# A four-layer graph network: one small product for two, later pair sums, kept loads on another queue, and half of a weight product at the end of the layer

## The chip, the cores and the metric

The kernel runs on one core of a Trainium2 chip. The metric is the time of one execution in microseconds (us) on the device. A core has TensorE (PE, matrix products; PEld is its weight load), VectorE (DVE), ScalarE (ACT), GpSimd (POOL) and SyncE (SP). The last two issue nearly all the transfers here; each engine works through its own queue in order, and waits at the head of it.

## What is computed

Four layers over a graph of N = 2708 nodes with F = 512 features; `adj` is dense with some 1.2% ones. Each layer is `x = layernorm(x + layer(x, adj))`. The change touches layer 0 and one product that layer 3 uses:

```
# layer 0, H = 4 heads of D = 128; both patterns are adj, so att has one mask
Xw  = einsum('hnd,hde->hne', Xh, W)
sig = sigmoid(f1[:, :, None] + f2[:, None, :])        # f1, f2: (H, N)
att = masked_softmax(adj * sig, adj != 0)             # (H, N, N)
Xa  = att @ Xw                                        # encode
Xn  = batchnorm(Xa as (N, F), gamma, beta)
emb = batchnorm(elu(Xn @ Wm.T + bm) + Xn)             # encoder MLP
Y   = elu((att @ emb) @ W.T)                          # decode, same att
out = batchnorm(elu(Y @ Wd.T + bd) + Y)               # decoder MLP
# layer 3
a = (x @ Wq + bq) @ (x @ Wk + bk).T / sqrt(512) + adj + adj
out = softmax(a) @ (x @ Wv + bv)
```

The kernel computes layer 3's scores from the merged weights `Wq Wk^T / sqrt(512)`, and it makes these within layer 0 and stores them to DRAM (`mqk_d`).

## The kernel before

**Tiles.** Features lie on 128 partitions in C = 4 chunks. The nodes are cut into NT = 22 blocks of up to 128 (the last has 20), and into two halves of 1354 columns, each in three parts of about 452 columns (a bank of PSUM takes 512). Heads go in two pairs.

**Attention passes.** `attention_pass` runs twice: encode (0 to about 572 us of the profile) and decode (about 693 to 1197 us). Each goes over half hf = 0, 1, over head pair p = 0, 1, and over the 22 blocks in the order `ORDER`. For each block the helper `form` loads the adjacency tile `a` (SP's queue, L358; 3 or 4 buffers), ScalarE makes the tanh of f1 + f2 for both heads of the pair (L385), VectorE multiplies with the mask (L393, one instruction of 128x2708), ScalarE takes the exponential (L394), and TensorE multiplies: six `po` products of 128x452 (L460). In encode, pass p = 0 also prepares the adjacency: VectorE makes `z` (tag z, one buffer, L374) and puts -1e30 where adj is 0 (L375), and GpSimd stores it to `adj_d`; the later passes load it from there. In decode VectorE counts the zeros of each column with another `z` (L335).

**Sums.** In encode TensorE also sums the exponentials over the nodes: `psm`, eight products of 128x340 (L483). For p = 1 most blocks are taken in pairs: VectorE adds two blocks' t (L477) and one `psm` does for both.

**Kept tiles.** Five block places of each pass (`KEPT`) have their finished `t` stored in DRAM in encode (GpSimd's queue, L442) and loaded again in decode in place of being formed (L445: 16 transfers of 1354 KB and 12 of 211.6 KB, on SP's queue). `t` has four buffers; a load waits until TensorE has read what the buffer held before.

**At a pass's end** (`keep`, in encode) the sums in PSUM are copied to `ft`, by VectorE and ScalarE in turn (L569). After pass (half 0, pair 1) `small_product` (L535 to L540) multiplies the encoder weights by the batch norm's beta: four products of 128x1 by 128x512, a copy of the row to SBUF (`row`, with the buffer of tag z), and four of 1x128 by 1x1, which turn it into a column; L575 adds the MLP's bias. Next to it VectorE clips the sums (L580), and the reciprocals go through DRAM (`few`, L589) and back as `rb`; the scaling and its statistics are done one by one behind the next pass's blocks.

**MLP stage** (about 572 to 693 us). Batch norm's scale and mean; wq and wk loaded and turned on TensorE (`tp_w`, L657); enc_w scaled in place (L677 on VectorE for two chunks, ScalarE for two); the sixteen products of the merged weights (L685, `ps_m`), copied to the tile `emb`'s free end by ScalarE and stored by GpSimd (L694); a small product `ps_u`; then for the six column chunks 4x4 products `ps_mlp` (L713), with a second small product `ps_mean` behind the first of them (the mean of the batch norm times the scaled weights, taken from the bias), elu (L499 to L508), and the turning of the result into rows (`tp_emb`, L745). Meanwhile the first decode blocks are formed, so VectorE has z and L393 of decode between the elus, and `linked` (L801), which needs the loads of `rb`.

**End of layer 0.** The last pass's sums go through `decode`'s tail: `ps_dec` (L848) and its elu; batch norm's scale and shift (L518 to L529, `bn_scale`, `bn_shift`). Layer 1 begins with a memset of one block of `hid_hi` (L955) and a copy of the centred weights (L965, `w_sb`), both ordered behind the shift; ScalarE applies the batch norm (L972), VectorE adds x (L979), TensorE turns the result (`tp_out`, L985) and multiplies (`ps_hid`, L117). Layer 1's tiles take the memory of layer 0's pools.

What is issued in which order is set by a list scheduler when the kernel is built, by each instruction's estimated readiness and the order of the program; `issue_after` puts a floor under it. The queues then run in that order.

Of the kernel before, what the change touches and what calls it, by code (L numbers as in the profile page):

```python
# [17 lines left out]
P = 128  # L18
# [11 lines left out]
def gnn_stack_kernel(  # L30
# [123 lines left out]
    mqk_d = dram.tile([C, P, C, P], F32, name="mqk_d")  # L154
    qscale = float(1.0 / F**0.5)
# [4 lines left out]
    with ExitStack() as l0:  # L160
# [160 lines left out]
        def attention_pass(values, first, att, psum, finish, f1b=None, blocks=(), spread=None, rest=None, taken={}):  # L321
# [83 lines left out]
            for hf, (h0, w) in enumerate(HSPAN):  # L405
                for p in range(H // HP):
# [13 lines left out]
                    before = None  # L420
                    for place, jt in enumerate(ORDER):
# [21 lines left out]
                        else:  # L443
                            for r in range(0, P if n == P else HB * Q, P if n == P else Q):
                                nc.sync.dma_start(t[r : r + n, :, :w], kept[:n, :, :w])  # L445
                            if p == 0 and jt in KEPT[1]:
                                count(hf, jt, att)
                        if po is None:


                            both = [
                                psum.tile([P, HP, BANK], F32, tag=f"po{q}", name="po", bufs=1)
                                for q in range(HB)
                            ]
                            po = [both[q][:, k, :] for k in range(HP) for q in range(HB)]
                        for k in range(HP):
                            h = HP * p + k
                            for q, (q0, qw) in enumerate(HCH[hf]):
                                r = 0 if n == P else q * Q
                                nc.tensor.matmul(  # L460
                                    po[HB * k + q][:, :qw],
                                    values[r : r + n, jt, h * P : (h + 1) * P],
                                    t[r : r + n, k, q0 : q0 + qw],
                                    start=(place == 0),
                                    stop=(place == NT - 1),
                                )
# [3 lines left out]
                        if prepare or not ALONE <= place < NT - LAST:  # L470
                            whole, m = t, n
                        elif place % 2 == 0:
                            before = t
                            continue
                        else:
                            whole, m = before, P
                            nc.vector.tensor_tensor(  # L477
                                whole[:n, :, :w], whole[:n, :, :w], tv, ALU.add
                            )
                        for k in range(HP):  # L480
                            for r, (q0, qw) in enumerate(SCH[hf]):

                                nc.tensor.matmul(  # L483
                                    sums[k][32 * r : 32 * r + 32, :SW],
                                    ones32[:m],
                                    whole[:m, k, q0 + qw - SW : q0 + qw],
                                    start=(place == 0),
                                    stop=(place == NT - 1),
                                )
# [62 lines left out]
        with (  # L552
# [8 lines left out]
            def keep(hf, p, po, sums):  # L561
# [10 lines left out]
                if hf == 0 and p == 1:  # L572
                    row = att.tile([P, HW], F32, tag="z", name="row", bufs=1)[:1, :F]
                    ps = small_product(po[0], mlp_w[0], prm_sb[:, B_ENC, :], row)
                    nc.vector.tensor_tensor(bias[:, 0, :], ps, prm_sb[:, MB_ENC, :], ALU.add)  # L575
# [55 lines left out]
            scale1, mean1 = batch_scale(stats, G_ENC, "bn1")  # L631

# [30 lines left out]
        with (  # L663
# [3 lines left out]

            (enc_w,) = mlp_w  # L670
            for c in range(C):
# [9 lines left out]
            mqk = emb[:, NT - 3 * C : NT - 2 * C, :]  # L681
            for c in range(C):
                ps = psum.tile([P, F], F32, tag="misc", name="ps_m", bufs=2)
                for o in range(C):
                    nc.tensor.matmul(  # L685
                        ps,
                        wqT[:, o, c * P : (c + 1) * P],
                        wkT[:, o, :],
                        start=(o == 0),
                        stop=(o == C - 1),  # L690
                    )
                nc.scalar.activation(mqk[:, c, :], ps, AF.Copy, scale=qscale)
            for o in range(C):
                nc.gpsimd.dma_start(mqk_d[o], mqk[:, :, o * P : (o + 1) * P])  # L694

            row = emb[:1, NT - 3 * C - 2 : NT - 3 * C, :]
# [8 lines left out]
            for ci, (c0, w) in enumerate(CHUNKS):  # L705
                pss = []
                for o in range(C):
# [13 lines left out]
                    if ci == 0 and o == 0:  # L721
                        pm = small_product(
                            psum.tile([P, F], F32, tag="misc", name="ps_mean", bufs=2),
                            enc_w,
                            mean1,
                            row[:, 1, :],
                        )
                        nc.vector.tensor_tensor(bias[:, 0, :], bias[:, 0, :], pm, ALU.subtract)
                        nc.vector.tensor_scalar(
                            bias[:, 1, :], bias[:, 0, :], 1.0, None, ALU.subtract  # L730
                        )
# [27 lines left out]
            spare = []  # L759

# [35 lines left out]
            def decode(hf, p, po, rb):  # L796
# [45 lines left out]
                def mlp(q, o, st, wide):  # L842
# [4 lines left out]
                    for c in range(C):  # L847
                        nc.tensor.matmul(  # L848
# [73 lines left out]
                for q in range(HB):  # L922
# [10 lines left out]
                    mlp(q, 3, st, True)  # L933

# [770 lines left out]
```

## Time and profile before

| | us |
|---|---|
| runs shown: median (lowest to highest of 3) | 3321.99 (3317.25 to 3322.62) |
| profiled execution: time | 3319.34 |
| profiled execution: span of the trace | 3317.5 |
| encode, 0 to 572: TensorE busy | 540.7 of 572 |
| MLP stage, 572 to 693 | 116.0 of 121 |
| decode, 693 to 1197 | 491.6 of 504 |
| layer 1, 1197 to 1510 | 304.3 of 313 |
| layers 2 and 3, to the end | 1780.1 of 1807.5 |

The span is the time from the first to the last instruction in the trace; 1.8 us of the execution lie around it. The granted clock of TensorE is 0.99 over the span. A row of a group reads: line, engine, operation, tile written and read, shapes, number; then busy time, mean ns of one; then idle time of the engine just before them and what ended it. A row of the waits reads: the engine and line that waited, what it waited for, us in all, times, the longest. A product in float32 stands as two records.

### The profile page before, as it was taken

The page shows a single profiled execution, that of the slowest core. Times are in us where ns is not written, and L with a number is a line of the kernel's source. Part 1 is how long each engine was busy: PE and PEld are TensorE (multiplying, and loading weights), DVE is VectorE, ACT ScalarE, POOL GpSimd, SP SyncE. Part 2 cuts the span into 40 slices and gives each one's busy share as a digit, 9 for nine tenths or more (in the row PEclk, how much of TensorE's full clock was granted, in tenths as well). Part 3 has the DMA queues.
Part 4 walks back from the last instruction along what each step waited for, and adds up shares of the span by engine and source line. Part 5 has one row for each costly group of instructions (what it writes and reads, how often), then busy time and mean ns, then how long its engine had stood idle before and what let it go on. Part 6 is the DMA issues. An engine that isn't in the chain of part 4 may idle for free.

```text
span 3317.5 us, 30401 instructions
## 1 busy us (share of the span) xinstructions
PE 3232.7 (97%) x10920; PEld 1725.2 (52%) x10920; DVE 1971.7 (59%) x3221; ACT 1319.5 (40%) x1497; POOL 130.1 (4%) x211
## 2 busy tenths in 40 slices
PE   8998999999999999999999999999999999999999
PEld 5443444454444446885554555444455555555554
DVE  7877977767687685445135667776353443543533
ACT  6887887457868652001133333332021010110111
POOL 1100100000000000000010000000000000000000
PEclk9999999999999999999999999999999999999999
DMA  8855863335555412540044444553211111111100
GB/s 289 299 189 169 310 214 123 105 108 199 177 176 175 161 40 84 144 123 15 1 127 128 119 124 134 148 148 108 69 46 34 42 34 42 40 32 45 36 24 20
DMA packets 172550, 381.45 MB, mean 115 GB/s; under 512 B 20938, under 2 KB 115094, under 8 KB 167982
## 3 DMA queue, kind: packets, MB, share of 16 engines
q1 hardware_dynamic: 156926, 308.16, 30.7%
q0 software_dynamic: 15472, 71.33, 5.8%
q8 instruction: 86, 1.41, 0.2%
q14 instruction: 66, 0.54, 0.1%
HBM read 307.22 MB, written 71.67 MB: 114 GB/s over the span
## 4 chain that ended last, share of the span: by engine, by line
PE 76%; DVE 9%; issue 8%; DMA 4%; ACT 3%; POOL 0%; SPq 0%; DVEq 0%; POOLq 0%; ACTq 0%
PE po L1310 22%; PE ps_s L1203 17%; PE po L460 11%; PE ps_nb L1044 6%; PE ps_wide L1105 4%; DVE t L393 3%; PE ps_hid L117 2%; PE ps_sup L1447 2%; PE ps_o L1388 2%; PE ps_mlp L713 2%; PE ps_dec L848 2%; DMA a<-adj_d 1%; ACT t L394 1%; DMA a_cols<-in_adjT_dram 1%; PE psm L483 1%
## 5 line engine op out<-in xcount | busy, mean ns | idle before, releaser
L393 DVE SCALAR_TENSOR_TENSOR t<-t,a 128x2708 f32<-128x2708 f32 (+1 forms) x156 | 462.1, 2974 | 125.0 <-ACT t L385 121.1
L385 ACT ACTIVATE t<-f1b,f2h 128x1354 f32<-128x1354 f32 (+1 forms) x312 | 428.1, 1413 | 61.7 <-PE po L460 28.0
L460 PE MATMUL po<-t,xw 128*128 128x452 f32 (+3 forms) x1056 | 415.1, 557 | 15.7 <-ACT t L394 15.7
L394 ACT ACTIVATE t<-t 128x2708 f32<-128x2708 f32 (+1 forms) x156 | 382.5, 2454 | 110.5 <-DVE t L393 110.3
L1310 PE MATMUL po<-sup,e 128*128 128x512 f32 x882 | 412.4, 602 | 6.2 <-DVE e L1500 5.9
L460 PE MATMUL po<-t,emb 128*128 128x452 f32 (+3 forms) x1056 | 400.3, 547 | 12.4 <-ACT t L394 9.1
L1310 PE MATMUL po<-e,xs 128*128 128x384 f32 (+1 forms) x1176 | 407.5, 489 | 0.0
L1203 PE MATMUL ps_s<-sup,hT 128*128 128x384 f32 (+1 forms) x1176 | 406.9, 490 | 0.0
L1581 DVE SCALAR_TENSOR_TENSOR e<-a_cols,ps_s 128x384 f32<-128x384 f32 (+1 forms) x154 | 85.6, 556 | 428.9 <-PE ps_s L1203 405.9
L460 PEld LDWEIGHTS po<-t,xw 128*128 128x128 f32 (+1 forms) x1056 | 191.2, 192 | 228.4 <-issue 201.7
L1203 PEld LDWEIGHTS ps_s<-sup,hT 128*128 128x128 f32 x1176 | 221.9, 190 | 164.2 <-issue 14.1
L460 PEld LDWEIGHTS po<-t,emb 128*128 128x128 f32 (+1 forms) x1056 | 193.5, 190 | 212.1 <-issue 187.3
L1310 PEld LDWEIGHTS po<-e,xs 128*128 128x128 f32 x1176 | 221.6, 190 | 157.2 <-issue 6.0
L1310 PEld LDWEIGHTS po<-sup,e 128*128 128x128 f32 x882 | 162.1, 192 | 173.9 <-issue 142.8
L1203 PE MATMUL ps_s<-hT 128*128 128x384 f32 (+5 forms) x672 | 212.3, 461 | 2.4 <-DVE e L1497 1.7
L97 ACT ACTIVATE ln_rstd<-ln_rstd 128x1 f32<-128x1 f32 x88 | 17.2, 201 | 495.0 <-DVE ln_rstd L96 494.7
L1496 ACT ACTIVATE a_cols<-a_cols,neg_big 128x384 f32<-128x384 f32 (+1 forms) x154 | 94.7, 616 | 239.0 <-DMA a_cols<-in_adjT_dram 190.7
L1044 PE MATMUL ps_nb<-hid_hi,at 128*128 128x512 f32 x484 | 185.6, 390 | 1.1 <-DVE at L1037 1.1
L1044 PE MATMUL ps_nb<-hid_lo,at 128*128 128x512 f32 x462 | 179.9, 389 | 0.0
L1305 DVE TENSOR_TENSOR acc<-acc,e 128x384 f32<-128x384 f32 (+2 forms) x294 | 162.4, 552 | 11.7 <-ACT e L1295 2.0
L1203 PEld LDWEIGHTS ps_s<-hT 128*128 128x128 f32 x672 | 122.4, 190 | 88.3 <-issue 17.3
L1294 DVE TENSOR_TENSOR e<-e,nmax 128x384 f32<-128x384 f32 (+1 forms) x308 | 154.5, 551 | 21.8 <-ACT nmax L1287 21.8
(247 smaller groups left out, 3316.8 us busy)
## 6 DMA issues: line engine op xcount, KB each, us to landing
a<-adj_d SPq DMA_DIRECT2D x110, 677.0 KB
a_cols<-in_adjT_dram SPq DMA_DIRECT2D x378, 192.0 KB
a<-in_adjT_dram SPq DMA_DIRECT2D x42, 677.0 KB
adj_d<-a POOLq DMA_DIRECT2D x42, 677.0 KB, 6.0
raw<-in_adjT_dram SPq DMA_DIRECT2D x105, 256.0 KB
kept<-t POOLq DMA_DIRECT2D x16, 1354.0 KB, 6.9
t<-kept SPq DMA_DIRECT2D x16, 1354.0 KB
a_cols<-in_adjT_dram SPq DMA_DIRECT2D x63, 202.0 KB
```

The costliest lines, as they stand in the source:

```text
L385: nc.scalar.activation(tv[:, k, :], f1b[:n, k, :w], AF.Tanh, bias=f2h[:n, jt, h : h + 1], scale=0.5,)
L393: step = nc.vector.scalar_tensor_tensor(tv, tv, GUARD, ab, ALU.add, ALU.mult)
L394: nc.scalar.activation(tv, tv, AF.Exp, scale=0.5)
L460: nc.tensor.matmul(po[HB * k + q][:, :qw], values[r : r + n, jt, h * P : (h + 1) * P], t[r : r + n, k, q0 : q0 + qw], start=(place == 0), ...
L1044: nc.tensor.matmul(pos[it], at, half[:, jt, :], start=(jt == 0 and k == 0), stop=(jt == NT - 1),)
L1105: nc.tensor.matmul(ps[:, :width], w(c, o), xt(c), start=(c == 0), stop=(c == C - 1),)
L1203: nc.tensor.matmul(ps[:, b * P : w], keys[:, c, j0 : j0 + P], st["q"][:, c, b * P :], start=(c == 0), stop=(c == C - 1),)
L1294: nc.vector.tensor_tensor(e, e, st["nmax"][:, :w], ALU.add)
L1305: nc.vector.tensor_tensor(acc, acc, e[:m], ALU.add)
L1310: nc.tensor.matmul(out, lhsT, rhs, start=(k == 0), stop=(k == NT - 1))
L1496: nc.scalar.activation(a, a, AF.Identity, bias=neg_big[: a.shape[0]], scale=1.0e30)
L1581: nc.vector.scalar_tensor_tensor(e, a, 2.0, ps, ALU.mult, ALU.add)
```

## The change

- The small product in `keep` goes, and `ps_mean` too. In their place one: `batch_shift` forms shift = beta - mean * scale of the encoder's batch norm, and `ps_shift` multiplies the weights with it, before they are scaled.
- The merged weights' products are in a helper, `merged(c)`. Chunks 0 and 1 of the four are made where all were. Then the turned weights wkT and half of wqT are stored to DRAM (`wkT_d`, `wqT_d`; 1 MB and 0.5 MB, GpSimd's queue). At the end of `decode` they are loaded into the two buffers of tag f1b (SP's queue), the other eight products go into two banks of `po` behind the last `ps_dec`, ScalarE copies them to a buffer of tag a, and GpSimd stores them to `mqk_d`, in four transfers of half the size.
- The loads of kept tiles are issued by GpSimd.
- The sums of a pair of blocks, and the addition before them, go into the helper `add_up`, which the program calls one block later: behind the next block's `form`, ahead of its `po` products.

```diff
--- before.py
+++ after.py
@@ -1,3 +1,4 @@
+from functools import partial
 from contextlib import ExitStack, nullcontext
 
 import concourse.bass as bass
@@ -152,6 +153,9 @@
     dram = ctx.enter_context(tc.tile_pool(name="dram", bufs=1, space=bass.MemoryType.DRAM))
     adj_d = dram.tile([N, N], F32, name="adj_d")
     mqk_d = dram.tile([C, P, C, P], F32, name="mqk_d")
+
+    wqT_d = dram.tile([P, C, C // 2 * P], F32, name="wqT_d")
+    wkT_d = dram.tile([P, C, F], F32, name="wkT_d")
     qscale = float(1.0 / F**0.5)
     uq = const.tile([P, C], F32, name="uq")
 
@@ -417,7 +421,7 @@
                     sums = None
                     if first and rest is None:
                         sums = sum_tiles()
-                    before = None
+                    before = waiting = None
                     for place, jt in enumerate(ORDER):
                         n = BLOCKS[jt][1]
 
@@ -442,7 +446,7 @@
                                 nc.gpsimd.dma_start(kept[:n, :, :w], tv)
                         else:
                             for r in range(0, P if n == P else HB * Q, P if n == P else Q):
-                                nc.sync.dma_start(t[r : r + n, :, :w], kept[:n, :, :w])
+                                nc.gpsimd.dma_start(t[r : r + n, :, :w], kept[:n, :, :w])
                             if p == 0 and jt in KEPT[1]:
                                 count(hf, jt, att)
                         if po is None:
@@ -453,6 +457,9 @@
                                 for q in range(HB)
                             ]
                             po = [both[q][:, k, :] for k in range(HP) for q in range(HB)]
+                        if waiting is not None:
+                            waiting()
+                            waiting = None
                         for k in range(HP):
                             h = HP * p + k
                             for q, (q0, qw) in enumerate(HCH[hf]):
@@ -467,26 +474,36 @@
                         if not first:
                             continue
 
-                        if prepare or not ALONE <= place < NT - LAST:
-                            whole, m = t, n
-                        elif place % 2 == 0:
+
+
+                        single = prepare or not ALONE <= place < NT - LAST
+                        if not single and place % 2 == 0:
                             before = t
                             continue
+
+                        def add_up(whole, m, more, first_one, last_one):
+                            if more is not None:
+                                nc.vector.tensor_tensor(
+                                    whole[: more.shape[0], :, :w],
+                                    whole[: more.shape[0], :, :w],
+                                    more,
+                                    ALU.add,
+                                )
+                            for k in range(HP):
+                                for r, (q0, qw) in enumerate(SCH[hf]):
+
+                                    nc.tensor.matmul(
+                                        sums[k][32 * r : 32 * r + 32, :SW],
+                                        ones32[:m],
+                                        whole[:m, k, q0 + qw - SW : q0 + qw],
+                                        start=first_one,
+                                        stop=last_one,
+                                    )
+
+                        if single:
+                            add_up(t, n, None, place == 0, place == NT - 1)
                         else:
-                            whole, m = before, P
-                            nc.vector.tensor_tensor(
-                                whole[:n, :, :w], whole[:n, :, :w], tv, ALU.add
-                            )
-                        for k in range(HP):
-                            for r, (q0, qw) in enumerate(SCH[hf]):
-
-                                nc.tensor.matmul(
-                                    sums[k][32 * r : 32 * r + 32, :SW],
-                                    ones32[:m],
-                                    whole[:m, k, q0 + qw - SW : q0 + qw],
-                                    start=(place == 0),
-                                    stop=(place == NT - 1),
-                                )
+                            waiting = partial(add_up, before, P, tv, False, False)
                     later += finish(hf, p, po, sums if first else rb) or []
             for work in later:
                 work()
@@ -569,10 +586,6 @@
                         taken[q % 2] = copy(
                             ft[:, HP * p + k, h0 + q0 : h0 + q0 + qw], po[HB * k + q][:, :qw]
                         )
-                if hf == 0 and p == 1:
-                    row = att.tile([P, HW], F32, tag="z", name="row", bufs=1)[:1, :F]
-                    ps = small_product(po[0], mlp_w[0], prm_sb[:, B_ENC, :], row)
-                    nc.vector.tensor_tensor(bias[:, 0, :], ps, prm_sb[:, MB_ENC, :], ALU.add)
                 sm = [att.tile([P, BW], F32, tag="rs", name="sm") for _ in range(HP)]
                 if not final:
                     for k in range(HP):
@@ -629,6 +642,7 @@
 
             attention_pass(xw, True, att, psum, keep, f1b, blocks, spread, rest, taken)
             scale1, mean1 = batch_scale(stats, G_ENC, "bn1")
+            shift1 = batch_shift(scale1, mean1, B_ENC, "bn1")
 
 
             emb = rows_tile("emb")
@@ -665,21 +679,9 @@
             tc.tile_pool(name="ps_c", bufs=1, space=PSUM) as psum,
         ):
 
-
-
-            (enc_w,) = mlp_w
-            for c in range(C):
-                if c % 2:
-                    nc.scalar.activation(
-                        enc_w[:, c, :], enc_w[:, c, :], AF.Copy, scale=scale1[:, c : c + 1]
-                    )
-                else:
-                    nc.vector.tensor_scalar(
-                        enc_w[:, c, :], enc_w[:, c, :], scale1[:, c : c + 1], None, ALU.mult
-                    )
-            stats = stats_tile("stats_b", NCH)
             mqk = emb[:, NT - 3 * C : NT - 2 * C, :]
-            for c in range(C):
+
+            def merged(c):
                 ps = psum.tile([P, F], F32, tag="misc", name="ps_m", bufs=2)
                 for o in range(C):
                     nc.tensor.matmul(
@@ -690,10 +692,38 @@
                         stop=(o == C - 1),
                     )
                 nc.scalar.activation(mqk[:, c, :], ps, AF.Copy, scale=qscale)
+
+            merged(0)
+
+
+            (enc_w,) = mlp_w
+
+            row = emb[:1, NT - 3 * C - 2 : NT - 3 * C, :]
+            pm = small_product(
+                psum.tile([P, F], F32, tag="misc", name="ps_shift", bufs=2),
+                enc_w,
+                shift1,
+                row[:, 1, :],
+            )
+            nc.vector.tensor_tensor(bias[:, 0, :], pm, prm_sb[:, MB_ENC, :], ALU.add)
+            nc.vector.tensor_scalar(bias[:, 1, :], bias[:, 0, :], 1.0, None, ALU.subtract)
+            for c in range(C):
+                if c % 2:
+                    nc.scalar.activation(
+                        enc_w[:, c, :], enc_w[:, c, :], AF.Copy, scale=scale1[:, c : c + 1]
+                    )
+                else:
+                    nc.vector.tensor_scalar(
+                        enc_w[:, c, :], enc_w[:, c, :], scale1[:, c : c + 1], None, ALU.mult
+                    )
+            stats = stats_tile("stats_b", NCH)
+            nc.gpsimd.dma_start(wkT_d, wkT)
+            nc.gpsimd.dma_start(wqT_d, wqT[:, :, half * P :])
+            merged(1)
             for o in range(C):
-                nc.gpsimd.dma_start(mqk_d[o], mqk[:, :, o * P : (o + 1) * P])
-
-            row = emb[:1, NT - 3 * C - 2 : NT - 3 * C, :]
+                nc.gpsimd.dma_start(
+                    mqk_d[o][:, :half, :], mqk[:, :half, o * P : (o + 1) * P]
+                )
             pu = small_product(
                 psum.tile([P, F], F32, tag="misc", name="ps_u", bufs=2),
                 wkT,
@@ -718,17 +748,6 @@
                             stop=(c == C - 1),
                         )
                     pss.append(ps)
-                    if ci == 0 and o == 0:
-                        pm = small_product(
-                            psum.tile([P, F], F32, tag="misc", name="ps_mean", bufs=2),
-                            enc_w,
-                            mean1,
-                            row[:, 1, :],
-                        )
-                        nc.vector.tensor_tensor(bias[:, 0, :], bias[:, 0, :], pm, ALU.subtract)
-                        nc.vector.tensor_scalar(
-                            bias[:, 1, :], bias[:, 0, :], 1.0, None, ALU.subtract
-                        )
                 for o in range(C):
                     dst = ft[:, o, c0 : c0 + w]
                     r = elu(
@@ -757,6 +776,7 @@
             dec_w = load_mlp(dec_wT, "dec_w")
             links = {}
             spare = []
+            last_dec = [None]
 
             def centre(pm):
 
@@ -845,7 +865,7 @@
                     q0, qw = HCH[hf][q]
                     ps = psum.tile([P, BANK], F32, tag="misc", name="ps_dec", bufs=2)
                     for c in range(C):
-                        nc.tensor.matmul(
+                        last_dec[0] = nc.tensor.matmul(
                             ps[:, :qw],
                             dec_w[:, c, o * P : (o + 1) * P],
                             t[:, c, q0 : q0 + qw],
@@ -931,6 +951,36 @@
                     if q == 0:
                         centre(po[0])
                     mlp(q, 3, st, True)
+
+
+                rest = [
+                    att.tile([P, HP, HW], F32, tag="f1b", name=name, bufs=2).rearrange(
+                        "p k w -> p (k w)"
+                    )
+                    for name in ("wk_again", "wq_again")
+                ]
+                wk_again = rest[0][:, : C * F].rearrange("p (c o) -> p c o", c=C)
+                wq_again = rest[1][:, : C * half * P].rearrange("p (c o) -> p c o", c=C)
+                nc.sync.dma_start(wk_again, wkT_d)
+                nc.sync.dma_start(wq_again, wqT_d)
+                mqk = att.tile([P, HW], F32, tag="a", name="mqk_rest", bufs=3)[:, : half * F]
+                mqk = mqk.rearrange("p (c o) -> p c o", c=half)
+                with tc.issue_after(last_dec[0].ins):
+                    for c in range(half):
+                        for o in range(C):
+                            nc.tensor.matmul(
+                                po[1 + c],
+                                wq_again[:, o, c * P : (c + 1) * P],
+                                wk_again[:, o, :],
+                                start=(o == 0),
+                                stop=(o == C - 1),
+                            )
+                for c in range(half):
+                    nc.scalar.activation(mqk[:, c, :], po[1 + c], AF.Copy, scale=qscale)
+                for o in range(C):
+                    nc.gpsimd.dma_start(
+                        mqk_d[o][:, half:, :], mqk[:, :, o * P : (o + 1) * P]
+                    )
 
             attention_pass(emb, False, att, psum, decode)
         dsum = small.tile([P, NT], F32, tag="dsum", name="dsum")
```

Lines of the changed kernel stand from 1 to 50 lines further down than those of the kernel before: L445 is L449, L460 is L467, L955 is L1005, L965 is L1015, L985 is L1035. `small_product` is as it was.

## The prediction

> **What bounds the kernel now.** I read the busy shares first, then the chain, then TensorE's waits, and then one window for each edit. The page's busy shares and its chain:
>
> ```profile
> PE 3232.7 (97%) x10920; PEld 1725.2 (52%) x10920; DVE 1971.7 (59%) x3221; ACT 1319.5 (40%) x1497; POOL 130.1 (4%) x211
> ...
> PE 76%; DVE 9%; issue 8%; DMA 4%; ACT 3%; POOL 0%; SPq 0%; DVEq 0%; POOLq 0%; ACTq 0%
> ```
>
> TensorE is busy for 3232.7 of 3317.5 us. So the change is worth what it takes out of TensorE's work, or out of the 85 us in which it is not busy, and nothing else counts. The list of TensorE's waits says where the larger pieces of those lie (time in all, times, longest):
>
> ```profile
> PE po L460 <- ACT t L394: 24.8, 13, 8.2
> PE tp_out L985 <- DVE ot L979: 7.5, 1, 7.5
> ...
> PE psm L483 <- DVE t L477: 3.7, 3, 1.4
> PE po L460 <- DVE ot L814: 3.2, 1, 3.2
> PE ps_u L540 <- DVE emb L538: 1.4, 1, 1.4
> ```
>
> Two waits stand out: 8.2 us for a masked exponential at a boundary between two passes (the first row's longest), and 7.5 us at the end of layer 0 (second row). The 3.7 us of pair sums are three waits.
>
> **1. The small product after pass (half 0, pair 1) goes.** TensorE's lines in the window 296 to 314 us:
>
> ```profile
> L460 PE MATMUL po<-t,xw 128*128 128x452 f32 (+1 forms) x8 | 4.3, 666 | 8.2 <-ACT t L394 8.2
> L535 PE MATMUL po<-enc_w,prm_sb 128*1 128x512 f32 x8 | 3.6, 592 | 0.0
> ...
> L540 PE MATMUL po<-ones,row 1*128 1x1 f32 x8 | 1.0, 248 | 0.8 <-DVE row L538 0.8
> ```
>
> The product occupies TensorE from 299.14 us, and the next pass's first po starts at 312.80: 3.6 + 0.8 + 1.0 + 8.2 = 13.7 us. VectorE is the reason for the 8.2. Its waits from 280 to 320 us:
>
> ```profile
> DVE ft L569 <- PE po L460: 9.5, 2, 9.2
> DVE row L538 <- PE po L535: 2.7, 1, 2.7
> ...
> DVE enc_bias L575 <- PE po L540: 1.1, 1, 1.1
> ```
>
> It sits idle 9.2 us for the old pass's sums, then 2.7 and 1.1 us inside the small product, and only then masks the new pass's adjacency (0.87 + 1.57 us) and multiplies (2.91 us): `row` has the only buffer of tag z, which the mask needs as well. Without `row` the build puts the first block's mask and product and the second's z ahead of the evacuations, into the 9.2 us. Its inputs are there: the tanh of two blocks ends at 288.8 us. Block 0 is then ready near 295 us, before TensorE's last old sum at 299.14. Later blocks cost VectorE 0.87 + 1.57 + 2.97 = 5.4 us, plus leftovers, against some 6.0 us on TensorE (its po and psm), so a stall of 0.5 to 1.5 us near the third or fourth is what I leave. The two other pass boundaries of this stage, at 172.9 and 445.1 us, show no gap. Gain 12 to 13.7 us at most; 8 if VectorE catches up slowly. I take **13 less 0.5 for late blocks: 12.5**. The replacement product of the shift (same 8 + 8 instructions) stands where `ps_mean`'s stood: no change in count.
>
> **2. Eight of the sixteen 128x512 products leave the MLP's start.** From 572 to 700 us the sixteen take 14.0 us (L685, 32 records, two to a product), so half is 7.0 us of TensorE's time. But VectorE is short of time there:
>
> ```profile
> DVE linked L801 <- DMA rb<-rs_d: 6.1, 1, 6.1
> DVE elu_r L506 <- ACT elu_m L501: 4.7, 5, 3.1
> DVE z L335 <- DMA a<-adj_d: 2.3, 1, 2.3
> ```
>
> Between 572 and 645 us it is busy 58.0 of 73, and its real slack appears only at 642 us (the 3.1). Products that start earlier meet a VectorE with the same 7 z, 4 multiplications of 2.97 us and the elus still to do, so the elus' evacuation holds the psum. Further, two new stores (1 MB and 0.5 MB, on GpSimd's queue) travel beside the loads that VectorE waits for here; by the page's rows a 1354 KB store takes 6.9 us to land and a 256 KB store 4.1, so I allow up to 2.5 us of delay for `linked` and z. The new shift product also makes the scaling of enc_w wait for a reader, 1.5 to 4 us later than before. Following both by hand: chunk 0's products end 5 us earlier, chunk 2's between 0.3 (loads late) and 3.3 us (not late) earlier. I take **2**, ends 0 and 3.5.
>
> **3. The same eight products return at the end of layer 0.** They fit into the wait of 7.5 us there: 8 x 0.87 = 7.0 us, directly behind the last ps_dec at 1197.3 us. So they cost nothing by themselves. What follows them does. Before, the timeline there reads:
>
> ```profile
> 1202.67 7.96 ACT L972 ACTIVATE ot<-ot,bn_shift,bn_scale 128x452 f32<-128x452 f32 x12 [0.84 <-DVE bn_shift L529]
> 1202.69 0.48 DVE L955 MEMSET hid_hi<- 128x512 f32 x1
> 1203.10 1.16 DVE L965 COPY w_sb<-xs 128x2048 f32<-128x2048 f32 x1
> 1204.17 3.85 DVE L979 TENSOR_TENSOR ot<-ot,xs 128x452 f32<-128x452 f32 x7
> ...
> 1204.84 0.47 PE L985 MATMUL tp_out<-ident,ot 128*128 128x128 f32 x1 [7.52 <-DVE ot L979]
> ```
>
> In the build of the changed kernel the memset waits for GpSimd's four last stores of mqk_d, because layer 1's tiles take the memory from which those stores read; the copy of the weights (w_sb) is queued behind it on VectorE, and ps_hid reads w_sb. The stores wait for two ScalarE copies out of po, the second behind four activations of L972 (0.66 us each): about 1205.9 us. Then four issues of some 0.65 us and a landing. The nearest rows are before's own four, issued from 602.42 to 604.38 and landed 605.74 to 611.15 us (median 4.1; 256 KB each, the new ones 128 KB), and the scores' stores (192 KB, 2.8). So the last lands at 1205.9 + 2.0 + 2.8..6.8 = 1210.7 to 1214.7, then 0.48 + 1.16, and ps_hid begins at 1212.4 to 1216.4 in place of 1205.2: 7.2 to 11.2 us late. The first transposes run meanwhile (0.4), and then VectorE's queue holds the row statistics behind the same memset, up to 2 us more. Layer 1's projection is bound by TensorE to 1490 us (no gap), so a delay is kept. I take **loss 8**. It could be nothing, if the stores are seen to have landed before the scale is ready, and 12 if the landing is slow and VectorE's backlog is the whole 2.
>
> **4. Kept loads move from SP's queue to GpSimd's** (16 of 1354 KB, 12 of 211.6 KB). SP's waits from 740 to 930 us:
>
> ```profile
> SPq L358 <- DVE t L393: 145.2, 28, 8.3
> SPq L445 <- PE po L460: 19.6, 4, 10.6
> ```
>
> A kept load waits for TensorE to free its t, and the adjacency loads behind it wait with it (19.6 us in four waits). VectorE in turn waits 19.1 us for such loads in that window, and TensorE loses 8.3 us to late exponentials there (5.8 at 795 us) and 3.2 at the evacuation L814, which stays. But at 784 to 796 us the adjacency load in front of the 5.8 waits for a multiplication (L393) to free its own buffer, not for a kept load; there the gain is only what earlier blocks bring. New costs: an issue on GpSimd takes 0.53 us (kept<-t, L442) where SP takes 0.32, and the landing, by the nearest row (6.9 us for a 1354 KB store from GpSimd), is longer than a block of the decode on TensorE; that is covered only because t has four buffers, so that a kept load can go out about three blocks ahead of its use. GpSimd has 1.05 us of work in the decode. I take **gain 3**, ends -3 (loads later) and +8.
>
> The Trainium skill speaks against this edit. "DMA: Bandwidth & Descriptors", section "Issuing engines are not separate DMA queues", says that transfers from all issuing engines share the same DMA engines and that a second issuer saves only the issue time. By that the edit is worth nothing on a path where SP's issue time is not late. The rows above show what that sentence leaves out: a queue whose head waits (10.6 us in one piece) holds what is behind it; so I keep a gain, but a small one. "SBUF — State Buffer" adds, in "The DVE blocks DMA trap", that descriptors made on GpSimd wait while VectorE runs a fast copy; no wait of that kind is in the rows of before.
>
> **5. Pair sums behind the next block.** The build has the same sequence of po and psm on TensorE in both kernels, and VectorE's additions in the same places but for the boundary. So the same three waits of psm for VectorE (3.7 us, shown at the top) stand where they stood: **0**; if they go after all, up to 3.7.
>
> **Sum**, against the profiled execution (3319.3 us; span 3317.5): -12.5 - 2 + 8 - 3 + 0 = -9.5, so 3309.8. The median of the runs shown is 3322.0, 2.7 above; I forecast **3310**, between the two bases (3309.8 and 3312.5).
>
> **Rivals.** (a) *The stall at the end is hidden*: the stores land before layer 1 asks, loss 0 to 2 in place of 8: 3319.3 - 12.5 - 2 + 1 - 3 = about 3303. For it: GpSimd is idle. Against: four stores behind a copy that is itself behind 2.6 us of activations. (b) *Nothing beside the boundary is gained*: VectorE gives back all of part 2 and the kept loads change nothing, and the end takes 9 to 10: 3319.3 - 12.5 + 9.5 = 3316. (c) *The other side*: kept loads on GpSimd's queue, whose head waits behind stores and copies of emb, arrive late. One late load stops TensorE for its excess over a block; 28 loads with 0.6 us each are 17 us, so 3310 + 3 + 17 = 3330. It decides from 0.4 us a load (11 us lost, 3324). (d) *The change doesn't do what it says* at pair sums: that is already in the sum, at 0; a gain there would give 3306.
>
> **How the numbers follow.** Forecast 0.45, (a) with (d) 0.25, (b) 0.17, (c) 0.13. A measurement of this kernel can tell about 0.2% (6.6 us) from no change. Faster holds the forecast, (a) and a small part of (b): 0.70. Same holds most of (b) and the mild end of (c): 0.18. Slower: 0.12. The range for 8 in 10 runs from 3298 (a with the kept loads' better end) to 3322 ((b) with both bad ends: 3319.3 - 12.5 + 12 + 3).
>
> **What would show it.** Right: no gap on TensorE from 299 to 312 us, first po of the pass right behind psm; memset of hid_hi 8 us or more after bn_shift with four mqk_d stores before it, and TensorE waiting there for w_sb; the row of SP's L445 gone; the elus of chunk 1 bound by VectorE. Wrong: a boundary that still waits for ACT t (then part 1 fails), or t of the kept blocks being waited for by TensorE (then part 4 has the wrong sign).

## The result, and the profile after

The change made the kernel slightly slower: 3329.11 us (median of 8 runs, 3327.89 to 3334.88) against 3322.13 (8 runs, 3317.25 to 3323.82), a ratio of 1.0027 with a 95% interval of 1.0016 to 1.0038. I had forecast 3310, in a range from 3298 to 3322.

TensorE's busy time hardly moved, and its waits did. First the page's busy shares, then the list of TensorE's waits of the changed kernel (us in all, times, longest):

```profile
PE 3232.2 (97%) x10904; PEld 1725.2 (52%) x10904; DVE 1972.2 (59%) x3221; ACT 1320.0 (40%) x1497; POOL 149.4 (4%) x245
```

```profile
PE po L467 <- ACT t L398: 40.8, 20, 6.6
PE ps_hid L118 <- DVE w_sb L1015: 5.5, 1, 5.5
...
PE psm L495 <- DVE t L486: 3.0, 3, 1.4
...
PE tp_out L1035 <- ACT mqk_rest L979: 1.7, 1, 1.7
```

The wait for ScalarE's exponential, which held the 8.2 us of the boundary before, did not shrink with it: it grew from 24.8 to 40.8 us. So waiting of that kind has come up somewhere else. The table says where; each entry is the length of a stage on TensorE in us, worked out from the starts and ends of its groups in the two traces.

| stage, by TensorE's own marks | before | after | difference |
|---|---|---|---|
| start to the last psm of encode | 572.3 | 557.5 | -14.8 |
| to the first po of decode (MLP stage) | 120.6 | 113.8 | -6.8 |
| to the last ps_dec (decode) | 504.4 | 530.9 | +26.5 |
| to the first ps_hid (change of layers) | 7.9 | 15.2 | +7.3 |
| to the last product | 2106.8 | 2103.5 | -3.3 |

The boundary's gap is gone. TensorE's lines in the window 296 to 314 us, after:

```profile
L467 PE MATMUL po<-t,xw 128*128 128x452 f32 (+1 forms) x37 | 15.0, 550 | 0.0
L495 PE MATMUL psm<-t,ones 128*32 128x340 f32 x48 | 4.1, 455 | 0.0
```

No small product stands between the passes, and the last column, the idle time before a group's instructions, is 0.0. But decode lost 26.5 us. VectorE's waits in decode, first in the kernel before, then after:

```profile
DVE t L393 <- ACT t L385: 78.1, 25, 5.7
DVE z L335 <- DMA a<-adj_d: 31.2, 13, 4.2
```

```profile
DVE z L339 <- DMA a<-adj_d: 76.9, 23, 8.5
DVE t L397 <- ACT t L389: 55.6, 17, 5.4
```

The count of zeros (z) waited 31 us for adjacency loads before, and 77 after. TensorE has no wait for a kept tile in its list: the kept loads, which were moved, are not late. What is late is the work of the blocks that are formed.

### The profile page after: what moved, and what is told of

It reads as the page before. It is cut to its first block, busy times and chain, and to the rows that moved or that the text cites. A ratio compares the mean times of both kernels' runs of the same rounds, so it can differ in the third digit from the quotient of the medians.

```text
span 3327.0 us, 30418 instructions
## 1 busy us (share of the span) xinstructions
PE 3232.2 (97%) x10904; PEld 1725.2 (52%) x10904; DVE 1972.2 (59%) x3221; ACT 1320.0 (40%) x1497; POOL 149.4 (4%) x245
## 4 chain that ended last, share of the span: by engine, by line
PE 59%; DVE 3%; DMA 1%; issue 0%; ACT 0%; SPq 0%; DVEq 0%; ACTq 0%
PE po L1360 22%; PE ps_s L1253 17%; PE ps_nb L1094 6%; PE ps_wide L1155 4%; PE ps_hid L118 2%; PE ps_sup L1497 2%; PE ps_o L1438 2%; DMA a_cols<-in_adjT_dram 1%; DVE e L1344 1%; PE tp L1145 0%; PE ps_s L1245 0%; DVE e L1550 0%; PE ps_parts L1277 0%; PE pb L1324 0%; DVE xs L1556 0%; DVE e L1547 0%
## 5 line engine op out<-in xcount | busy, mean ns | idle before, releaser
L397 DVE SCALAR_TENSOR_TENSOR t<-t,a 128x2708 f32<-128x2708 f32 (+1 forms) x156 | 461.8, 2975 | 104.7 <-ACT t L389 101.0
L467 PE MATMUL po<-t,emb 128*128 128x452 f32 (+3 forms) x1056 | 408.7, 555 | 30.5 <-ACT t L398 30.4
L398 ACT ACTIVATE t<-t 128x2708 f32<-128x2708 f32 (+1 forms) x156 | 382.5, 2454 | 114.1 <-DVE t L397 113.8
L467 PE MATMUL po<-t,xw 128*128 128x452 f32 (+3 forms) x1056 | 411.4, 552 | 10.5 <-ACT t L398 10.4
L467 PEld LDWEIGHTS po<-t,emb 128*128 128x128 f32 (+1 forms) x1056 | 197.0, 194 | 235.2 <-issue 191.8
L467 PEld LDWEIGHTS po<-t,xw 128*128 128x128 f32 (+1 forms) x1056 | 189.1, 190 | 221.6 <-issue 198.1
```

The costliest lines, as they stand in the source:

```text
L397: step = nc.vector.scalar_tensor_tensor(tv, tv, GUARD, ab, ALU.add, ALU.mult)
L398: nc.scalar.activation(tv, tv, AF.Exp, scale=0.5)
L467: nc.tensor.matmul(po[HB * k + q][:, :qw], values[r : r + n, jt, h * P : (h + 1) * P], t[r : r + n, k, q0 : q0 + qw], start=(place == 0), ...
```

## Experiments

Two theories stood after the traces. **A**: the kept loads on GpSimd's queue cost the 26.5 us. **B**: decode is paced by VectorE and the adjacency loads, so that the lead of 21.6 us which encode and MLP gave was lost there in any case. A splits in two: **A1**, the build orders VectorE's z and t otherwise when the loads are on that queue; **A2**, the transfers get in each other's way. In front of each diff stands the kernel that it starts from. The ratio is always to the kernel before on the same chip; the runs down to noend_pool were made on one chip and those from pool_order on another, so between the two groups ratios and stages are compared, not times.

No run undoes the later pair sums alone. In the traces, TensorE's order in the encode passes of noend_sp (below) and of the kernel before differs only around the small product, and psm waits for VectorE's additions 2.8 us in all, where it waited 3.7. So that part of the change did next to nothing.

**k_sp: the kept loads back on SP's queue.** From the changed kernel:

```diff
-                                nc.gpsimd.dma_start(t[r : r + n, :, :w], kept[:n, :, :w])
+                                nc.sync.dma_start(t[r : r + n, :, :w], kept[:n, :, :w])
```

> The changed kernel with the loads of kept tiles back on SP's queue, all else as changed. In the changed kernel the decode stage loses 26.5 us against before (TensorE stands 21.6 us ahead at the first po of decode and 4.9 behind at the last ps_dec). Theory A (the loads on GpSimd's queue are to blame, by the order of VectorE's work that the build makes with them or by the transfers): the decode loses 0 to 5 us, so the time is 3305 to 3310. Rival B (decode can't keep a lead, because VectorE and the loads of adjacency set its pace): it still loses 20 or more, time 3325 or more.

Measured: 3303.29 us, ratio 0.9959 (0.9946 to 0.9971), a little below what A gave. Decode takes 504.5 us, as before the change, and starts 19.6 us earlier than before. B falls: decode keeps a lead that it is handed.

**b_pool: the kernel before, with the one line the other way.**

> The kernel before with nothing but the loads of kept tiles moved to GpSimd's queue. Theory A: the decode gets 15 to 25 us longer, time 3337 to 3347. Rival B (decode gives back whatever lead it is handed): no lead is handed here, so within 5 us of before, 3317 to 3327.

Measured: 3341.42 us, ratio 1.0075 (1.0062 to 1.0088); decode 527.5 us, 23 more. The edit hands no lead over here, and the loss is nearly the same. A holds, and the line is enough by itself.

**noend_sp and noend_pool: all sixteen products of the merged weights at the start again.** From k_sp and from the changed kernel:

```diff
-            nc.gpsimd.dma_start(wkT_d, wkT)
-            nc.gpsimd.dma_start(wqT_d, wqT[:, :, half * P :])
-            merged(1)
+            for c in range(1, C):
+                merged(c)
...
-                wk_again = rest[0][:, : C * F].rearrange("p (c o) -> p c o", c=C)
...
```

> The changed kernel with the kept loads on SP's queue and all sixteen products of the merged weights at the start of the MLP stage: what is left of the change is the one small product for two and the pair sums. Against k_sp this undoes the move of half the products. Theory A2 (the move costs more at the end of layer 0 than it saves at the MLP stage, 7.3 us lost at the end and 6.8 saved at the start in the changed kernel): within 3 us of k_sp. Rival (the lead saved at the MLP stage is lost in decode, which the end then adds to): noend_sp is 5 us or more faster than k_sp, 3300 to 3305.

> The changed kernel with all sixteen products at the start of the MLP stage, the kept loads on GpSimd's queue. Theory A: the decode loss of some 20 us stays, since neither the MLP stage nor the end makes it: time 3322 to 3332. Rival C (the late decode comes from the two reloads of turned weights in SP's queue and the stores beside the decode's first loads): decode recovers, 3305 to 3312.

(A2 in the first of these two expectations stands for another theory, about the move of the products; elsewhere it is the transfers.) Measured: noend_sp 3306.30 us, ratio 0.9965 (0.9951 to 0.9979); noend_pool 3328.32, ratio 1.0033 (1.0020 to 1.0046). Their MLP stages are 120.4 and 120.3 us against k_sp's 113.3, and the change of layers 7.8 and 7.9 against 15.2: 7 us saved by the move, 7.3 lost. noend_sp is 3.0 us from k_sp, at the edge of what I gave for that. noend_pool's decode still takes 527.9 us, 23.5 more than before the change, so the reloads of the turned weights and the stores beside decode's first loads are not the cause of these. Since the pair sums did next to nothing, noend_sp is in effect the kernel before with one small product for two: 11.7 us faster by the medians.

**pool_order: GpSimd's queue, with VectorE's order of z and t held to SP's.** From the changed kernel; the list has 112 entries, the order of z and T in k_sp's build (T is the multiplication that writes t):

```diff
+DVE_ORDER = [
+    ('z', 0, 0),
+    ('T', 0, 0, 0),
...
+            if not first:
+                for u, v in zip(DVE_ORDER, DVE_ORDER[1:]):
+                    tc.add_manual_dep(
+                        made[v].ins,
+                        made[u].ins.name,
...
```

> The changed kernel, with the kept loads on GpSimd's queue as changed, but with VectorE's order of z and t (L339, L397) in decode held by hand to the order that the build makes with SP's loads (as in k_sp). Theory A1 (the loads on GpSimd lose time because the build gives VectorE another order of z and t, in which a z stands ahead of work that is ready and waits for its adjacency load): the decode loss goes, time 3303 to 3308, as k_sp's 3303. Rival A2 (the transfers themselves: kept loads that go out beside the adjacency loads slow these): the order does not help, 3322 to 3332.

Measured: 3307.83 us, ratio 0.9970 (0.9958 to 0.9981). The queue is the changed kernel's, and still decode takes 506.5 us instead of 530.9. VectorE's waits there:

```profile
DVE t L511 <- ACT t L503: 87.5, 27, 5.4
DVE z L453 <- DMA a<-adj_d: 25.2, 12, 4.0
```

The 77 us for adjacency are 25 again. With VectorE's order held, the build also sets ScalarE's order anew, but not in the first pass of decode (half 0, pair 0): there this trace and the changed kernel's have TensorE's, ScalarE's, GpSimd's and SP's instructions in the same order, and only VectorE's z and T differ. That pass takes 108.2 us, k_sp's 108.2 and the changed kernel's 118.4 (from its first po to the next pass's). So A1 is shown; of A2, with this order, there can be some 2 us in decode (506.5 against k_sp's 504.5), and that much is left.

**sp_order: the counterpart, SP's queue with the order of GpSimd's build.** The same edit on k_sp with the other list.

> The counterpart: k_sp (kept loads on SP's queue) with VectorE's order of z and t in decode held to the order that the build makes with GpSimd's loads. Theory A1: as slow as the changed kernel, 3322 to 3335. Rival A2: as k_sp, 3303 to 3308.

Measured: 3328.96 us, ratio 1.0038 (1.0025 to 1.0052), decode 531.7 us, as A1 said. It is the weaker of the two: its largest gap on TensorE (12.9 us at 725.6) has no match in the changed kernel, and SP's kept loads wait 89.1 us for TensorE, against 45.5 in k_sp. So here the order also works through SP's queue, and the equal total is partly chance.

**e_nostore: what makes the stall ahead of layer 1.** From k_sp, all sixteen products and stores at the start, and at the end:

```diff
-                for o in range(C):
-                    nc.gpsimd.dma_start(
-                        mqk_d[o][:, half:, :], mqk[:, :, o * P : (o + 1) * P]
-                    )
```

> k_sp with all sixteen products of the merged weights and their full stores at the start of the MLP stage, and the eight products at the end of layer 0 made a second time with their two copies by ScalarE, whose results are not stored. So it leaves out the four stores at the end, and TensorE makes eight products more in all. Theory: the stall ahead of layer 1 (15.2 us from the last ps_dec to the first ps_hid in k_sp, 7.9 in noend_sp) is the stores' landing, and goes to some 10 us without them; time 3306 + 2.5 = 3308 to 3310. Rival (the products and copies themselves make it): 13 to 15 us, time 3311 to 3314.

Measured: 3304.86 us, ratio 0.9966 (0.9953 to 0.9978), 10.4 us from the last ps_dec to the first ps_hid. The time is some 3 us below what I expected, less than the 4.4 us between this kernel's lowest and highest run; the stage is as expected. Of the 7.3 us lost, the stores make 4.8 (15.2 less 10.4) and the products and copies 2.6 (10.4 less 7.8).

**e_quarter: a quarter of the products at the end, in one store.** From k_sp (c = 3 alone, one copy, and):

```diff
+                nc.gpsimd.dma_start(
+                    mqk_d[:, :, C - 1, :].rearrange("o p j -> p o j"),
+                    mqk[:, 0, :].rearrange("p (o j) -> p o j", o=C),
+                )
```

> k_sp with a quarter instead of half of the merged weights at the end: four products of the sixteen, one copy by ScalarE ahead of the batch norm's scale, and one store in place of four. By the stall's arithmetic (copy at 4.1 us after the last ps_dec, one issue of 0.7, landing 2.3, memset and copy 1.6) ps_hid begins some 9 us after the last ps_dec, 1 later than without any product at the end, and the MLP stage is 3.4 shorter than noend_sp's: 2 us faster than noend_sp, about 3304, within 1 us of k_sp. Rival (the stall does not follow the stores): 14 us or more to ps_hid, 3309 or more.

Measured: 3299.81 us, ratio 0.9949 (0.9937 to 0.9962), the lowest ratio here, with an interval that overlaps k_sp's and noend_sp's. 9.1 us from ps_dec to ps_hid, as expected, and an MLP stage of 116.9 against noend_sp's 120.4. The two stages together take 126.0 us in this trace, 128.5 in k_sp's (half at the end) and 128.2 in noend_sp's (nothing at the end). The total is 4 us below what I expected; that lies in the layers behind, 2102.6 us against noend_sp's 2106.5 in the profiled executions, and is open. Its timeline at the end:

```profile
1184.07 0.60 ACT L978 ACTIVATE mqk_rest<-po 128x512 f32<-128x512 f32 x1 [1.02 <-PE po L971]
...
1184.96 0.79 POOL L979 DMA_DIRECT2D mqk_d<-mqk_rest  x1 [497.94 <-ACT mqk_rest L978]
...
1188.08 0.48 DVE L1004 MEMSET hid_hi<- 128x512 f32 x1
1188.48 1.16 DVE L1014 COPY w_sb<-xs 128x2048 f32<-128x2048 f32 x1
...
1189.70 2.07 PE L118 MATMUL ps_hid<-w_sb,ot 128*128 128x512 f32 x2 [0.93 <-DVE w_sb L1014]
```

The one copy goes ahead of the batch norm's scale, the one store has landed when VectorE comes to the memset, and TensorE waits 0.93 us for the weights where the changed kernel waits 5.5.

## Why the prediction was wrong

**The step that failed is part 4, the kept loads**: "I take **gain 3**, ends -3 (loads later) and +8". They cost some 23 us (b_pool, a ratio of 1.0075; and 1.0027 for the changed kernel against 0.9959 for k_sp). I had looked at the loads' waits in SP's queue and at what they hold up there, and had not asked whether the build keeps VectorE's order of z and t in decode when the loads change their queue. It doesn't; why the build turns the order round is not in the record. The pass of half 0, pair 0, by the two builds (numbers are blocks, T is the multiplication L397; blocks 4, 8, 21, 13 and 17 are kept):

```
SP:     z9 z10 T7 T9 T10 z21 z11 T11 z12 T12 z14 T14 z15 T15 z16 z18 T16
GpSimd: z9 z10 T7 z21 T9 T10 z11 z12 z14 T11 z15 T12 z16 T14 T15 z18 z19 T16
```

The adjacency tile has three buffers, and z and T of a block read the same one. With GpSimd's order z14 stands ahead of T11 and z15 ahead of T12, so a count that needs a tile not yet loaded stands in front of a multiplication that has all it needs. VectorE's timeline in the changed kernel:

```profile
721.59 1.57 DVE L339 TENSOR_SCALAR_CACHE_REDUCE z<-a 128x1354 uint8<-128x1354 f32 x1 [3.75 <-DMA a<-adj_d]
723.08 0.08 DVE L339 DVE_READ_ACCUMULATOR z<-a 128x1 f32 x1
723.08 2.97 DVE L397 SCALAR_TENSOR_TENSOR t<-t,a 128x2708 f32<-128x2708 f32 x1
732.52 1.57 DVE L339 TENSOR_SCALAR_CACHE_REDUCE z<-a 128x1354 uint8<-128x1354 f32 x1 [6.47 <-DMA a<-adj_d]
734.01 0.08 DVE L339 DVE_READ_ACCUMULATOR z<-a 128x1 f32 x1
734.01 2.97 DVE L397 SCALAR_TENSOR_TENSOR t<-t,a 128x2708 f32<-128x2708 f32 x1
```

These are z14, T11, z15, T12. T11's tanh ended at 718.5 us and it starts at 723.1, behind z14; T12's ended at 729.9 and it starts at 734.0, behind z15, whose load could go out only when T11 had freed a buffer (SP's queue: a<-adj_d at 726.08). TensorE has gaps of 3.45 and 3.33 us right there (725.1 and 736.2). Nobody in this pass waits for z itself: a count whose time does not matter holds up work whose time does. These two gaps are 6.8 us of the loss. In the next pass z of half 1, block 1 stands ahead of T20, which has had its tanh for 1.7 us when it starts; TensorE's 6.63 us at 903.9 follow there, but that chain was not followed step by step.

My reason for a gain failed as well. In pool_order the kept loads no longer stand in SP's queue, and the order is the good one: decode is 2 us longer than k_sp's, not shorter. Freeing the adjacency loads of the kept loads in front of them gained TensorE nothing in sum: most adjacency loads wait for their own buffer anyway (in k_sp's decode SP waits 299 us for VectorE's T to free one, and 45.5 for TensorE to free a t). Here the Trainium skill's rule that I weighed ("DMA: Bandwidth & Descriptors", section "Issuing engines are not separate DMA queues") was nearer to the truth than my exception to it: by the rule the move is worth the issue time alone, and pool_order shows no gain.

Rival (c) gave 3330 for kept loads on GpSimd's queue, 1 us from the result. Its mechanism, kept loads that arrive late, is not what happened, so its number is right by luck. The sign that I had named for a wrong part 4, TensorE waiting for t of kept blocks, did not appear either: part 4 failed without it.

**Part 1, the boundary, held.** I took 12.5; noend_sp, where it is the only part that acts, is 11.7 us faster than the kernel before by the medians. From pass start to pass start (first po to first po) noend_sp gains 13.7 us over the boundary (126.2 against 139.9), the upper end that I gave. The late blocks were mis-sized: I took 0.5 us, near the third or fourth, and the pass behind the boundary takes 136.0 us, where it took 132.3. In the changed kernel its gaps stand ahead of the seventh and the thirteenth block (1.0 and 2.3 us, at 334 and 368; before, one of 1.2 at 350). The last pass of encode makes up for it (123.7 us to the last psm, before 127.2), which was no part of my working; b_pool, unchanged there, shows 125.3, so half of that is scatter and the sum came out right partly by luck. The stage's length varies by 3 to 4 us between profiled executions of the same work (568.6 in b_pool, 572.3 before, the same code up to there), so the 14.8 of the table is no better figure than 11.7.

**Part 2, the MLP stage, was mis-sized**: "I take **2**", and it was 6.8 in the changed kernel and 7.0 between noend_sp and k_sp. TensorE's time for the eight products (7.0) was saved nearly whole. My argument that VectorE is short of time and gives it back was wrong here: the delay that I allowed for loads did not come. VectorE waited 1.3 us for `rb`, where it had waited 6.1.

**Part 3, the end, held**: loss 8 against 7.3 measured, and the mechanism by its own lines. But "they cost nothing by themselves" was not quite so: by e_nostore 2.6 of the 7.3 us are the products and their copies. The timeline of the changed kernel there:

```profile
1210.24 0.57 ACT L979 ACTIVATE mqk_rest<-po 128x512 f32<-128x512 f32 x1
...
1211.11 2.91 POOL L981 DMA_DIRECT2D mqk_d<-mqk_rest  x4 [93.44 <-ACT mqk_rest L979]
...
1215.80 0.48 DVE L1005 MEMSET hid_hi<- 128x512 f32 x1 [0.41 <-DMA mqk_d<-mqk_rest]
...
1216.20 1.16 DVE L1015 COPY w_sb<-xs 128x2048 f32<-128x2048 f32 x1
...
1217.41 5.28 PE L118 MATMUL ps_hid<-w_sb,ot 128*128 128x512 f32 x6 [5.45 <-DVE w_sb L1015]
```

Read down: the second copy, the four stores behind it, VectorE released by the last of them, the weights' copy, TensorE. (VectorE stood idle for only 0.41 us of this: the build had put other work ahead of the memset.) The stores took 2.2 us from issue to landing, a little under my lower end of 2.8. The move of half the products is worth about nothing in sum (7 saved, 7.3 lost; k_sp against noend_sp 3303.3 against 3306.3, with intervals of the ratio that overlap).

**Part 5, the pair sums, held**: 0 (psm waits 3.0 us for the additions, 3.7 before).

**The sum**, redone with what was measured in the traces: -14.8 - 6.8 + 26.5 + 7.3 - 3.3 = +8.9 us (the medians differ by 7.0). The last term, in the layers behind, stays open: the eight other kernels take between 0.2 and 4.2 us less there than the kernel before, with no pattern that I could tie to a part of the change. b_pool, whose program there is that of the kernel before, takes 1.9 us less in its profiled execution, so part of this can be scatter.

## What to carry to other kernels

Moving a transfer to another queue is not a local edit where a scheduler orders the engines: compare the order of every engine before and after, in every stage that shares its buffers, before pricing the transfer itself. In an order, look for an instruction that nobody waits for (a count, a statistic) standing ahead of one that is ready, when the first must wait for a buffer that has just come free; holding the order by hand, and comparing the other engines' order afterwards, tells this from a slow transfer in one run. Work put into a gap costs little by itself (2.6 us here, with its copies), but its results' stores can hold the memory that the next stage needs (4.8 us here): by the stages of the traces a quarter of it, in one store that starts early (e_quarter), was worth some 2 us more than half of it or none; in the total time this is not clear of the noise.

## What the runs showed of the hardware

Not all of the 26.5 us in decode is idle time. TensorE's gaps of over 0.2 us there grew from 12.3 to 30.4 us, 18.1, and the other 8.4 are products that took longer (busy 500.5 against 492.0 us in decode). They run at a lower granted clock: by an estimate from the traces' record of the clock, the half clock cost 11.2 us in decode while products ran, and 3.2 before the change. Much of it stands behind the longer gaps. Windows of the changed kernel, the first behind the gap of 3.45 us, the second behind one of 3.33, the third behind one of 6.54, the fourth behind one of 2.85, the last behind one of 6.63 (PEclk is the granted clock, the third number from the right):

```profile
728.60:732.00 3.40, 3.40 (x5) 1.73 (x6) 0.00 (x0) 1.26 (x1) 0.00 (x0) 0.50 0.66 264
739.50:743.00 3.50, 3.47 (x9) 1.82 (x10) 2.00 (x3) 3.50 (x3) 0.00 (x0) 1.00 0.22 89
789.80:793.00 3.20, 3.20 (x5) 1.53 (x6) 3.20 (x5) 0.00 (x0) 0.00 (x0) 0.50 0.52 217
...
899.00:902.40 3.40, 3.37 (x9) 1.82 (x10) 1.95 (x3) 3.40 (x2) 0.00 (x0) 1.00 0.81 279
910.50:914.00 3.50, 3.50 (x5) 1.80 (x6) 3.50 (x5) 1.26 (x1) 0.00 (x0) 0.50 0.64 203
```

Behind gaps of 3.45, 6.54 and 6.63 us the clock is 0.50, and five records run where nine do behind gaps of 2.85 and 3.33, at a clock of 1.00. In the window behind the first (732.0 to 736.2 us) it is 0.73; so, by an estimate from these two windows, the wait of 3.45 us cost some 2.8 us more than itself (0.5 of 3.4 and 0.27 of 4.2), and that of 3.33 nothing. "TensorE: Matmul & The Clock Gate", section "Part 1: The HAM clock gate (the "warmup" mystery)", of the Trainium skill states such a limit: half the clock after an idle window of some 3.4 us. In these five gaps it fits; elsewhere it does not. The first window here is of the changed kernel, behind a gap of 2.28 us in encode, the second of the kernel before, behind its gap of 3.21 us at 905.6:

```profile
370.80:374.20 3.40, 3.40 (x5) 1.72 (x6) 3.37 (x3) 2.90 (x2) 0.00 (x0) 0.50 0.84 339
```

```profile
908.80:912.20 3.40, 3.40 (x6) 1.51 (x7) 3.40 (x7) 3.40 (x3) 0.00 (x0) 0.64 0.50 190
```

The clock is 0.50 and 0.64 behind these shorter gaps, so the length of one gap does not decide it, and what does is open. I had counted waits by their length alone, without the slower products behind them; for the boundary too this left something out, with 0.57 behind its 8.2 us in the kernel before (312.8 to 316.3 us).
